# The last image's tail of a selective-scan block, run alone at the end: six pieces at a time, rows kept on chip

## The chip, the cores and the metric

The kernel runs on one core of a Trainium2 chip. The metric is the device time of one execution in microseconds (us), the median of several runs. A profile of one execution shows five engines: PE (matrix products; PEld is its weight load), DVE (vector), ACT (scalar functions), POOL (GpSimd) and SP, which here issues every DMA.

## The reference, cut to what matters

Eight images of 64 x 64 positions and 96 channels go through two layers. Layer 0 is a two-dimensional selective scan: normalise, project to 192 channels, convolve, scan along diagonals and antidiagonals in both directions (16 states for each channel), add the directions, normalise, gate, project back to 96 and add the input. Layer 1 is linear attention over the 4096 positions of an image, then a quantised feed-forward. What the change touches is what comes after the scans:

```python
y01 = ys[:, 0:2] + ys[:, 2:4][..., ::-1]
y = y01[:, 0][..., inv_d] + y01[:, 1][..., inv_a]       # diagonals + antidiagonals
yn = (y - mu) * rsqrt(var + 1e-05) * ln_w + ln_b
x = x + (yn * silu(z)) @ out_proj_w.T                   # layer 0 and its residual
t = x.reshape(8, 4096, 96)
t = t + attention(_ln_t(t))                             # no softmax: q (k^T v), 6 heads
t = t + ffn(_ln_t(t))                                   # 96 -> 384 -> 96, 8-bit floats
```

Since the attention has no softmax, all of it is one 97 x 96 matrix per image, made from the sum over all positions of the outer products of the normalised rows (the gram matrix, with a column of ones). No row can go on before every row of its image has been added to it.

## The kernel before, in words

The scans of the eight images run one after another in a loop over 8 x 16 blocks of 512 positions and 16 states, and use DVE, PE, ACT and POOL at once. Under the scans of image b, generators do the front of image b + 1 (`front`: normalise, convolve, lay out) and the tail of image b - 1 (`tail`). The last image's tail has no scan to lie under: it is put out after the loop, alone.

The order of instructions on each engine is written by a small planner, the class `Work`. A job is a generator; each `yield` names the engine of the next step (A for ACT, V for DVE, G for POOL, P for PE), with its cost and whether it needs a PSUM bank. `next` begins a round and starts the jobs that fit into a phase's width; `at` lets every job whose next step is on this engine put out that step, job after job. In the mode `alone`, which `finish` sets, a round goes through A, V, P and G once, with no regard to costs or due times: the jobs of a phase advance in lockstep, one stage a round, as far as banks go. Engines execute in the order written, so a stage of a later round stands behind the same engine's stages of all jobs of the earlier round.

`tail` has three phases over pieces of 512 positions (`NCH` = 8 pieces an image):

- `join` (L571): loads the two directions' sums y0 and y1 of a piece from the DRAM tensors `wide` (L582), the input rows t (L584) and the gate (L589). PE adds y0 and y1 by products with the identity into PSUM (L597), ACT copies the sum (L604), DVE takes statistics from PSUM (L607, L608). `rsqrt` (L353 to L362) makes scale and shift on ACT and POOL, ACT normalises (L613), PE turns the rows (L619), DVE multiplies by the gate (L621), PE makes the output product with the residual (L625, L633, L636). ACT copies it to t (L640), which is written to the DRAM tensor `mid` (L641). Statistics (L644), root, normalisation by POOL (L652), the gram product (L658) and its sum (L661, L663) follow; the turned rows (L669, L672) go to the DRAM tensor `turned` (L674), whose source lies in y1's buffer. Width 3, and piece c waits until piece c - 2 is through (`joined`). y0 and y1 have three buffers each.
- `attention` (L681): makes the 97 x 96 matrix (L685 to L703).
- `layers` (L710): loads the turned rows (L717) and t (L719) back, adds attention (L722, L727), copies (L731), takes statistics (L735, L736), root, normalises (L742), turns (L747), quantises (L750), makes the hidden layer (L756, ACT L758 and L759), quantises (L762), the second product (L767), copies (L772), and POOL adds (L775, L776). Width 3.

The banks that a tail may use at the end are `banks` (2) and `feed` (3); the three banks of the scans' sum y are not among them. The scans' memory is the pool `scan`, open to the end of the program. The loop ends with `place`, which writes the last block to `wide` (L1036).

The end of `run` before:

```python
work.free += [(f, -9) for f in feed]
work.stream(end(NB - 1))
work.finish(all_done)
```

Of the kernel before, what the change touches and what calls it, by code (L numbers as in the profile page):

```python
# [9 lines left out]
F32 = mybir.dt.float32  # L10
# [3 lines left out]
ALU = mybir.AluOpType  # L14
# [36 lines left out]
@with_exitstack  # L51
def hybrid_block(ctx, tc, x, out, w):


    nc = tc.nc
    NB = x.shape[0]
    const = ctx.enter_context(tc.tile_pool(name="const", bufs=1))
    dram = ctx.enter_context(tc.tile_pool(name="dram", bufs=4, space=DRAM))
    k = weights(tc, const, w)
    pool = ctx.enter_context(tc.tile_pool(name="scan", bufs=1))  # L60
    psum = ctx.enter_context(tc.tile_pool(name="psum", bufs=1, space=PSUM))
    with tc.manual_schedule():

        k.tables = lambda: nc.scalar.preload_act_table_set("natural_log_exp_and_others")
        run(tc, pool, psum, dram, x, out, k, NB)


def weights(tc, const, w):
# [487 lines left out]
        yield [walk(c) for c in range(NST)], 3  # L556


def tail(tc, work, x, out, k, at, b):

    nc = tc.nc
    area = dict(reuse_waits="tile")
    with tc.tile_pool(name=f"t1_{b}", bufs=1, **area) as p1:
        gram = p1.tile([DM + 1, DM + 1], F32, tag="gram", name="gram")
        grams = [0]

        with tc.tile_pool(name=f"t2_{b}", bufs=2, **area) as p2:

            joined = set()

            def join(c):  # L571
                s = slice(4 * c, 4 * c + 4)

                def tile(name, shape, bufs=2):
                    return p2.tile(shape, F32, tag=name, name=name, bufs=bufs)

                ys = [tile(f"y{d}", [P, 4, DI], 3) for d in range(2)]
                for y, src in zip(ys, at.wide):
                    rows = src[0 : HH * WIDE].rearrange("(n y x) -> y n x", y=2, x=WIDE)
                    for v in range(2):  # L580
                        rv = rows[v, s, WW * DI : 2 * WW * DI].rearrange("n (x c) -> x n c", c=DI)
                        nc.sync.dma_start(out=y[v * WW : (v + 1) * WW], in_=rv)  # L582
                t = tile("t", [P, 4, DM], 3)
                nc.sync.dma_start(out=t, in_=x[b].rearrange("(t p) c -> p t c", p=P)[:, s, :])  # L584
                yield "P", 0.0, 4, False
                while c >= 2 and c - 2 not in joined:
                    yield SPIN
                gate = tile("gate", [HC, 2, CH])
                nc.sync.dma_start(out=gate, in_=at.gate[:, :, c * CH : (c + 1) * CH])  # L589
                st, mv = tile("st", [P, 4, 6]), tile("mv", [P, 4, 2])  # L590
                yn = ys[0]
                for j in range(2):
                    ps = yield bank(0.65)
                    v = view(ps, P, 2, DI)
                    for i in range(2):
                        for d in range(2):
                            nc.tensor.matmul(  # L597
                                v[:, i, :], k.ident, ys[d][:, 2 * j + i, :],
                                start=(d == 0), stop=(d == 1), skip_group_check=True,
                            )  # L600
                        if i == 0:
                            yield pe(0.65)
                    yield act(0.5)
                    nc.scalar.copy(yn[:, 2 * j : 2 * j + 2, :], v)  # L604
                    yield dve(1.0, 0)
                    for i in range(2):
                        nc.vector.bn_stats(st[:, 2 * j + i, :], v[:, i, :])  # L607
                        nc.vector.bn_aggr(mv[:, 2 * j + i, :], st[:, 2 * j + i, :])  # L608
                    work.release(ps)
                r, m = yield from rsqrt(nc, p2, k, mv, P, 4, "n")  # L610
                yield act(1.4)
                for i in range(4):
                    nc.scalar.activation(yn[:, i, :], yn[:, i, :], AF.Identity, scale=r[:, i : i + 1], bias=m[:, i : i + 1])  # L613
                yg = tile("yg", [HC, 2, CH])
                for a in range(2):
                    ps = yield bank(0.45)
                    v = view(ps, HC, CH)
                    for i in range(4):
                        nc.tensor.transpose(v[:, i * P : (i + 1) * P], yn[:, i, a * HC : (a + 1) * HC], k.ident)  # L619
                    yield dve(0.7)  # L620
                    nc.vector.tensor_tensor(yg[:, a, :], v, gate[:, a, :], ALU.mult)  # L621
                    work.release(ps)
                ps = yield bank(0.65)
                po = view(ps, P, 4, DM)
                nc.tensor.matmul(  # L625
                    view(ps, P, 4 * DM), k.ident, t.rearrange("p a c -> p (a c)"), start=True, stop=False, skip_group_check=True
                )
                for i in range(4):
                    if i % 2 == 0:
                        yield pe(1.2)  # L630
                    tok = slice(i * P, (i + 1) * P)
                    for a in range(2):
                        nc.tensor.matmul(  # L633
                            po[:, i, :], yg[:, a, tok], k.w_ln[:, a, :], start=False, stop=False, skip_group_check=True
                        )
                        nc.tensor.matmul(  # L636
                            po[:, i, :], gate[:, a, tok], k.b_ln[:, a, :], start=False, stop=(a == 1), skip_group_check=True
                        )
                yield act(0.5)
                nc.scalar.copy(t, po)  # L640
                nc.sync.dma_start(out=at.mid[:, s, :], in_=t)  # L641
                yield dve(1.7, 0)
                for i in range(4):
                    nc.vector.bn_stats(st[:, i, :], po[:, i, :])  # L644
                    nc.vector.bn_aggr(mv[:, i, :], st[:, i, :])
                work.release(ps)
                r, m = yield from rsqrt(nc, p2, k, mv, P, 4, "a")
                xa = ys[0].rearrange("p a c -> p (a c)")[:, 0 : 4 * (DM + 1)].rearrange("p (a c) -> p a c", a=4)
                yield gp(1.6)
                nc.gpsimd.memset(xa[:, :, DM : DM + 1], 1.0)  # L650
                for i in range(4):
                    nc.gpsimd.tensor_scalar(xa[:, i, 0:DM], t[:, i, :], r[:, i : i + 1], m[:, i : i + 1], ALU.mult, ALU.add)  # L652


                ps = yield bank(0.65)
                v = view(ps, DM + 1, DM + 1)
                for i in range(4):
                    nc.tensor.matmul(v, xa[:, i, :], xa[:, i, :], start=(i == 0), stop=(i == 3))  # L658
                yield dve(0.3)
                if grams[0] == 0:  # L660
                    nc.vector.tensor_copy(gram, v)  # L661
                else:
                    nc.vector.tensor_tensor(gram, gram, v, ALU.add)  # L663
                grams[0] += 1
                work.release(ps)
                ps = yield bank(0.45)
                v = view(ps, DM + 1, CH)
                for i in range(4):
                    nc.tensor.transpose(v[:, i * P : (i + 1) * P], xa[:, i, :], k.ident)  # L669
                xaT = ys[1].rearrange("p a c -> p (a c)")[0 : DM + 1, 0:CH]  # L670
                yield act(0.6)
                nc.scalar.copy(xaT, v)  # L672
                work.release(ps)
                nc.sync.dma_start(out=at.turned[:, c * CH : (c + 1) * CH], in_=xaT)  # L674
                joined.add(c)

            yield [join(c) for c in range(NCH)], 3

        att = SimpleNamespace()

# [24 lines left out]

        yield [attention()], 1

        with tc.tile_pool(name=f"t3_{b}", bufs=3, **area) as p2:

            def layers(c):  # L710
                s = slice(4 * c, 4 * c + 4)

                def tile(name, shape, dtype=F32):
                    return p2.tile(shape, dtype, tag=name, name=name)

                xaT = tile("xaT", [DM + 1, CH])
                nc.sync.dma_start(out=xaT, in_=at.turned[:, c * CH : (c + 1) * CH])  # L717
                t = tile("t", [P, 4, DM])
                nc.sync.dma_start(out=t, in_=at.mid[:, s, :])  # L719
                ps = yield bank(0.65, 4)  # L720
                po = view(ps, P, 4, DM)
                nc.tensor.matmul(  # L722
# [53 lines left out]
                nc.gpsimd.tensor_tensor(t, t, y16, ALU.add)  # L776
                nc.sync.dma_start(out=out[b].rearrange("(t p) c -> p t c", p=P)[:, s, :], in_=t)

            yield [layers(c) for c in range(NCH)], 3


def run(tc, pool, psum, dram, x, out, w, NB):

# [4 lines left out]


    nc = tc.nc
    steps = [
        (b, q, c) for b in range(NB) for q in range(2) for c in (range(NST) if q == 0 else range(NST - 1, -1, -1))
    ]
# [291 lines left out]
    for i in range(total + LAG + 1):  # L1087
# [34 lines left out]
        if i + 4 < total:  # L1122
            fetch(i + 4)
        feeds.pop(i, None)
    work.free += [(f, -9) for f in feed]
    work.stream(end(NB - 1))
    work.finish(all_done)


# [75 lines left out]
```

## Time and profile before

| | us |
|---|---|
| median of 3 runs | 12146.02 |
| lowest, highest | 12140.42, 12148.66 |
| the profiled execution | 12157.04 |
| its span, first to last instruction | 12155.1 |

| engine | busy us | share of the span |
|---|---|---|
| PE | 9958.7 | 82% |
| PEld | 8012.1 | 66% |
| DVE | 9683.1 | 80% |
| ACT | 9501.2 | 78% |
| POOL | 9737.6 | 80% |

How to read the lines below. The slices cut the span in 40 equal parts; a digit is the busy share in tenths, PEclk the TensorE clock that was granted, in tenths of full speed. A line of the timeline has the start in us, the time, the engine, the line of the code, the operation, out<-in, shapes and count. A line of the chain of waits has the start, the time and what the chain was in. A line of the stage windows has a stretch, its length, busy us (and instructions) of PE, PEld, DVE, ACT and POOL, then the granted clock (1.00 is full), the DMA engines' busy share and GB/s.

### The profile page before, as it was taken

To read this page: it belongs to the slowest core of one execution; us is meant where nothing else is said; L and a number is where in the kernel's file an instruction comes from. 1 tells how busy PE (TensorE), PEld (TensorE's weight loads), DVE (VectorE), ACT (ScalarE), POOL (GpSimd) and SP (SyncE) were. 2 spreads that over 40 slices of the span, in tenths; PEclk is the share of its full clock that TensorE was granted. 3 is DMA by queue.
4 is the path that set the end of the run, shared out by engine and by line. 5 is a ranking of instruction groups with operands and counts; after the bars stand their busy time and mean duration, and the time that the engine had idled before them with its cause. 6 is when DMAs were issued, how large, how long until landed. Compare 5 with 4: busy or idle time off the path is not lost.

```text
span 12155.1 us, 187007 instructions
## 1 busy us (share of the span) xinstructions
PE 9958.7 (82%) x62804; PEld 8012.1 (66%) x62804; DVE 9683.1 (80%) x11092; ACT 9501.2 (78%) x19842; POOL 9737.6 (80%) x6927
## 2 busy tenths in 40 slices
PE   4698889888898888988888888988889888888874
PEld 3476667666676666766677666766667666666653
DVE  1488998878888888888888888888888878888971
ACT  1588888877888788877888878887788878878862
POOL 0588998878988788888888889888898888889972
PEclk9799999998998989989899999999989899988985
DMA  2334333533335433353333433344333443322331
GB/s 53 91 92 124 100 93 94 136 104 96 94 88 134 112 94 93 90 141 101 95 90 106 127 102 95 90 127 117 92 92 93 132 108 93 100 87 84 100 93 42
DMA packets 1138471, 1213.47 MB, mean 100 GB/s; under 512 B 464998, under 2 KB 744167, under 8 KB 1137511
## 3 DMA queue, kind: packets, MB, share of 16 engines
q1 hardware_dynamic: 1137510, 1201.51, 36.0%
q8 instruction: 499, 8.18, 0.3%
q14 instruction: 462, 3.78, 0.1%
HBM read 877.94 MB, written 323.09 MB: 99 GB/s over the span
## 4 chain that ended last, share of the span: by engine, by line
PE 29%; ACT 22%; DVE 20%; POOL 11%; issue 9%; SPq 4%; DMA 4%; DVEq 0%; POOLq 0%; ACTq 0%
DVE h L958 13%; ACT feedT L937 8%; PE y L993 7%; PE feed L945 7%; ACT decay L923 6%; POOL h L979 6%; DVE feed L962 4%; PE bank L493 3%; DMA cc<-crow 2%; PE bank L835 2%; SPq L538 2%; PE bank L877 1%; POOL delta L874 1%; PE feed L947 1%; PE bank L858 1%
## 5 line engine op out<-in xcount | busy, mean ns | idle before, releaser
L979 POOL TENSOR_TENSOR h<-h,cc 128x1536 f32<-128x1536 f32 x2048 | 7073.1, 3454 | 401.7 <-DMA cc<-crow 205.0
L958 DVE TENSOR_TENSOR_SCAN h<-decay,carry,feed 128x512 f32<-128x512 f32 x5376 | 6500.6, 1261 | 623.0 <-PE feed L945 510.4
L923 ACT ACTIVATE decay<-delta,a_neg 128x512 f32<-128x512 f32 x6144 | 3976.8, 713 | 1303.6 <-DVE h L958 1298.1
L945 PE MATMUL feed<-ident,feedT 128*128 128x128 f32 x15360 | 2738.5, 303 | 1508.3 <-DVE h L958 1237.9
L993 PE MATMUL y<-ident,h 128*128 128x128 f32 x24576 | 3804.4, 289 | 68.6 <-ACT ys L1021 37.3
L937 ACT ACTIVATE feedT<-duT,rows 128x192 f32<-128x192 f32 x10240 | 3670.8, 443 | 1.6 <-PE feed L945 1.1
L993 PEld LDWEIGHTS y<-ident,h 128*128 128x128 f32 x24576 | 3154.2, 151 | 527.5 <-issue 483.4
L945 PEld LDWEIGHTS feed<-ident,feedT 128*128 128x128 f32 x15360 | 1970.4, 155 | 2118.5 <-DVE h L958 667.9
L962 DVE TENSOR_TENSOR feed<-feed,du 128x512 f32<-128x512 f32 x2304 | 1442.5, 687 | 210.7 <-PE feed L947 205.8
L974 POOL COPY carry<-h 128x3 f32<-128x3 f32 x2048 | 395.4, 193 | 1065.4 <-DVE h L958 985.8
L958 DVE TENSOR_TENSOR_SCAN h<-decay,feed 128x512 f32<-128x512 f32 x768 | 883.9, 1202 | 102.5 <-PE feed L945 83.2
L493 PE MATMUL bank<-wf,xp 97*128 97x192 f32 x4320 | 873.6, 334 | 1.7 <-ACT xp L458 1.7
L947 PE MATMUL feed<-x,pick 77*128 77x512 f32 x1536 | 846.4, 633 | 0.7
L493 PEld LDWEIGHTS bank<-wf,xp 97*128 97x128 f32 x4320 | 704.8, 195 | 28.8 <-issue 15.9
L879 DVE SCALAR_TENSOR_TENSOR delta<-bank,delta 128x512 f32<-128x512 f32 x381 | 258.5, 678 | 287.0 <-POOL delta L874 159.6
L886 POOL TENSOR_TENSOR du<-delta,u 128x1536 f32<-128x1536 f32 x128 | 449.4, 3511 | 10.6 <-DVE delta L879 10.6
L877 PE MATMUL bank<-x,ws 13*128 13x512 f32 x762 | 439.4, 657 | 20.8 <-DVE delta L879 20.8
L872 POOL TENSOR_TENSOR e<-e,duT 128x1536 f32<-128x1536 f32 x128 | 441.9, 3452 | 16.7 <-ACT delta L865 16.6
L858 PE MATMUL bank<-x,ws 13*128 13x512 f32 x766 | 436.6, 650 | 17.3 <-ACT x L848 17.3
L874 POOL TENSOR_TENSOR delta<-delta,e 128x1536 f32<-128x1536 f32 x128 | 441.0, 3446 | 0.1
L947 PEld LDWEIGHTS feed<-x,pick 77*128 77x128 f32 x1536 | 261.0, 201 | 152.7 <-issue 96.2
L835 PE MATMUL bank<-wx,u 128*128 128x77 f32 x3048 | 356.5, 273 | 0.0
(260 smaller groups left out, 8885.1 us busy)
## 6 DMA issues: line engine op xcount, KB each, us to landing
cc<-crow SPq DMA_DIRECT2D x4096, 128.0 KB
u<-seq SPq DMA_DIRECT2D x256, 384.0 KB
wide<-ys SPq DMA_DIRECT2D x512, 192.0 KB
ut<-image SPq DMA_DIRECT2D x768, 64.0 KB
seq<-us SPq DMA_DIRECT2D x128, 384.0 KB
part<-ys SPq DMA_DIRECT2D x64, 768.0 KB
y<-part SPq DMA_DIRECT2D x64, 768.0 KB
y<-wide SPq DMA_DIRECT2D x256, 192.0 KB
```

The lines of the kernel that those rows point to most:

```text
L493: nc.tensor.matmul(v[:, j, :], flat[:, o : o + P], k.wf[:, i, :], start=(i == 0), stop=(i == 8), skip_group_check=True)
L835: nc.tensor.matmul(v[:, j, :], u[:, g, j * P : (j + 1) * P], w.wx[:, q, g, :], start=(g == 0), stop=(g == G - 1))
L874: nc.gpsimd.tensor_tensor(delta, delta, e, ALU.add)
L877: nc.tensor.matmul(ps, w.ws[:, q, g, :], x[0 : 2 * NR + 1, :], start=True, stop=True)
L923: nc.scalar.activation(decays[i][:, g, :], made[m].delta[:, g, :], AF.Exp, scale=w.a_neg[:, q, g, n : n + 1])
L937: nc.scalar.activation(f[part], o.duT[part], AF.Copy, scale=scale)
L945: nc.tensor.transpose(feed[g][:, j * P : (j + 1) * P], feeds[i][:, j * G + g, :], w.ident)
L947: nc.tensor.matmul(feed[0], w.pick[:, FEED[:n].count("D"), :], made[m].x, start=True, stop=True)
L958: nc.vector.tensor_tensor_scan(h[:, g, back], a[:, g, back], feed[g][:, back], init, ALU.mult, ALU.add)
L962: nc.vector.tensor_tensor(feed[g], feed[0], made[m].du[:, g, :], ALU.mult)
L979: nc.gpsimd.tensor_tensor(hs[i], hs[i], c.unsqueeze(1).to_broadcast([P, G, T]), ALU.mult)
L993: nc.tensor.matmul(y[:, j, :], hs[i][:, g, r * P : (r + 1) * P], w.ident, is_transpose=True, start=(n == 0 and j % 4 == 0), stop=(n == NS ...
```

## The change

The last image's tail is called with `last=True`, after the scans' pool is closed, and differs in this:

- `join` and `layers` run at width 6 with six buffers, without the wait for piece c - 2; `join` starts at DVE's step at once, and a piece loads y0, y1, t and its gate in this order.
- The directions are added by DVE from memory, in place in y0, and the statistics are taken there; L597 and L604 are not put out.
- t and the turned rows of all eight pieces stay on chip (`kept`); `mid` and `turned` are neither written nor read.
- The scans' sum y gives three more banks: eight in all.

The tails of the other images are as before.

```diff
-    pool = ctx.enter_context(tc.tile_pool(name="scan", bufs=1))
...
-def tail(tc, work, x, out, k, at, b):
+def tail(tc, work, x, out, k, at, b, last=False):
...
+        kept = {}
-        with tc.tile_pool(name=f"t2_{b}", bufs=2, **area) as p2:
+        with tc.tile_pool(name=f"t2_{b}", bufs=6 if last else 2, **area) as p2:
...
-                t = tile("t", [P, 4, DM], 3)
+                t = p1.tile([P, 4, DM], F32, tag=f"t{c}", name="t") if last else tile("t", [P, 4, DM], 3)
...
-                yield "P", 0.0, 4, False
-                while c >= 2 and c - 2 not in joined:
+                if not last:
+                    yield "P", 0.0, 4, False
+                while not last and c >= 2 and c - 2 not in joined:
                     yield SPIN
...
-                for j in range(2):
+                if last:
+                    yield dve(2.5)
+                    nc.vector.tensor_tensor(yn, ys[0], ys[1], ALU.add)
+                    for i in range(4):
+                        nc.vector.bn_stats(st[:, i, :], yn[:, i, :])
+                        nc.vector.bn_aggr(mv[:, i, :], st[:, i, :])
+                for j in range(0 if last else 2):
...
-                nc.sync.dma_start(out=at.mid[:, s, :], in_=t)
+                if not last:
+                    nc.sync.dma_start(out=at.mid[:, s, :], in_=t)
...
-                xaT = ys[1].rearrange("p a c -> p (a c)")[0 : DM + 1, 0:CH]
+                if last:
+                    xaT = p1.tile([DM + 1, CH], F32, tag=f"xaT{c}", name="xaT")
+                else:
+                    xaT = ys[1].rearrange("p a c -> p (a c)")[0 : DM + 1, 0:CH]
...
+                if last:
+                    kept[c] = t, xaT
+                else:
+                    nc.sync.dma_start(out=at.turned[:, c * CH : (c + 1) * CH], in_=xaT)
...
-            yield [join(c) for c in range(NCH)], 3
+            yield [join(c) for c in range(NCH)], 6 if last else 3
...
-        with tc.tile_pool(name=f"t3_{b}", bufs=3, **area) as p2:
+        with tc.tile_pool(name=f"t3_{b}", bufs=6 if last else 3, **area) as p2:
...
+                if last:
+                    t, xaT = kept[c]
+                else:
...
-            yield [layers(c) for c in range(NCH)], 3
+            yield [layers(c) for c in range(NCH)], 6 if last else 3
...
+    scans = ExitStack()
+    pool = scans.enter_context(tc.tile_pool(name="scan", bufs=1))
...
-    work.free += [(f, -9) for f in feed]
-    work.stream(end(NB - 1))
+    work.finish(all_done)
+    scans.close()
+    y = psum.tile([P, TB * G, P], F32, tag="y", name="y_end").rearrange("p (b k) c -> p b (k c)", b=G)
+    work.free += [(f, -9) for f in feed] + [(y[:, g, :], -9) for g in range(G)]
+    work.stream(tail(tc, work, x, out, w, image(NB - 1), NB - 1, True))
     work.finish(all_done)
```

More of the change, by code (lines that the diff above doesn't have):

```diff
@@ L64, in hybrid_block @@
         k.tables = lambda: nc.scalar.preload_act_table_set("natural_log_exp_and_others")
-        run(tc, pool, psum, dram, x, out, k, NB)
+        run(tc, psum, dram, x, out, k, NB)
 def weights(tc, const, w):
@@ L574, in tile @@
                 def tile(name, shape, bufs=2):
-                    return p2.tile(shape, F32, tag=name, name=name, bufs=bufs)
+                    return p2.tile(shape, F32, tag=name, name=name, bufs=6 if last else bufs)
                 ys = [tile(f"y{d}", [P, 4, DI], 3) for d in range(2)]
@@ L590, in join @@
                 st, mv = tile("st", [P, 4, 6]), tile("mv", [P, 4, 2])
+                yg = tile("yg", [HC, 2, CH]) if last else None
                 yn = ys[0]
-                for j in range(2):
+                if last:
[5 more added lines that the diff above has]
+                for j in range(0 if last else 2):
                     ps = yield bank(0.65)
@@ L613, in join @@
                     nc.scalar.activation(yn[:, i, :], yn[:, i, :], AF.Identity, scale=r[:, i : i + 1], bias=m[:, i : i + 1])
-                yg = tile("yg", [HC, 2, CH])
+                yg = yg or tile("yg", [HC, 2, CH])
                 for a in range(2):
@@ L673, in join @@
                 work.release(ps)
-                nc.sync.dma_start(out=at.turned[:, c * CH : (c + 1) * CH], in_=xaT)
+                if last:
+                    kept[c] = t, xaT
+                else:
+                    nc.sync.dma_start(out=at.turned[:, c * CH : (c + 1) * CH], in_=xaT)
                 joined.add(c)
-            yield [join(c) for c in range(NCH)], 3
+            yield [join(c) for c in range(NCH)], 6 if last else 3
         att = SimpleNamespace()
@@ L714, in tile @@
                     return p2.tile(shape, dtype, tag=name, name=name)
[L716 to L719, printed above, removed]
+                if last:
+                    t, xaT = kept[c]
+                else:
+                    xaT = tile("xaT", [DM + 1, CH])
+                    nc.sync.dma_start(out=xaT, in_=at.turned[:, c * CH : (c + 1) * CH])
+                    t = tile("t", [P, 4, DM])
+                    nc.sync.dma_start(out=t, in_=at.mid[:, s, :])
                 ps = yield bank(0.65, 4)
@@ L777, in layers, with run @@
                 nc.sync.dma_start(out=out[b].rearrange("(t p) c -> p t c", p=P)[:, s, :], in_=t)
-            yield [layers(c) for c in range(NCH)], 3
-def run(tc, pool, psum, dram, x, out, w, NB):
+            yield [layers(c) for c in range(NCH)], 6 if last else 3
+def run(tc, psum, dram, x, out, w, NB):
     nc = tc.nc
+    scans = ExitStack()
+    pool = scans.enter_context(tc.tile_pool(name="scan", bufs=1))
     steps = [
```

## The prediction

> **What bounds the kernel now.** The page's forty slices come first; one slice is 12155.1 / 40 = 304 us.
>
> ```profile
> PE   4698889888898888988888888988889888888874
> DVE  1488998878888888888888888888888878888971
> PEclk9799999998998989989899999999989899988985
> ```
>
> From the second slice to the third last, scans keep DVE, PE, ACT and POOL 70 to 90% busy. In the last slice DVE is busy a tenth and the TensorE clock is at half: the last image's tail runs there alone, and there no engine is the limit. The timeline of SP's queue and of POOL dates it.
>
> ```profile
> 11779.32 6.39 SPq L1036 DMA_DIRECT2D wide<-ys  x8
> 11785.88 3.76 SPq L582 DMA_DIRECT2D y<-wide  x4
> ...
> 11823.37 1.64 POOL L652 TENSOR_SCALAR y<-t,ar,am 128x96 f32<-128x96 f32 x4
> ...
> 11827.09 1.64 POOL L652 TENSOR_SCALAR y<-t,ar,am 128x96 f32<-128x96 f32 x4
> ...
> 11977.88 0.24 ACT L703 COPY w_att<-feed 97x96 f32<-97x96 f32 x1 [1.29 <-PE feed L700]
> ```
>
> The scans' last result leaves at 11779, the tail's first load is issued at 11785.9, the attention matrix is ready at 11978.1, the span ends at 12155.1. So `join` with the attention takes 192 us and `layers` 177: 369 us, 3% of the span, and the change touches nothing else. POOL takes 3.72 us a piece for the second normalisation (11823.37 to 11827.09). Next, the chain inside this stretch:
>
> ```profile
> 11881.37 10.16 DMA turned<-y
> 11891.55 0.57 SPq L582
> ...
> 11925.42 10.18 DMA turned<-y
> 11935.62 0.57 SPq L582
> ...
> 11995.13 16.64 DMA t<-mid
> ...
> 12056.10 17.32 DMA t<-mid
> ...
> 12110.27 16.47 DMA t<-mid
> ```
>
> Two of `join`'s four pairs wait 10 us for the write of `turned` before their own y loads may start (y1 holds the turned rows). Each of the three groups of `layers` first waits for `mid` and `turned` to come back. Why so long? The stage windows (us; PE, PEld, DVE, ACT, POOL busy; clock, DMA share, GB/s):
>
> ```profile
> 11794.00:11796.00 2.00, 1.91 (x6) 1.43 (x6) 0.00 (x0) 0.45 (x1) 0.00 (x0) 0.50 1.14 230
> ...
> 11830.00:11832.00 2.00, 2.00 (x10) 2.00 (x9) 0.00 (x0) 1.17 (x2) 0.00 (x0) 0.50 0.01 3
> 11832.00:11834.00 2.00, 2.00 (x12) 2.00 (x11) 0.20 (x1) 0.48 (x1) 0.00 (x0) 0.84 0.07 13
> ...
> 11836.00:11838.00 2.00, 0.00 (x0) 0.00 (x0) 0.14 (x1) 0.00 (x0) 0.19 (x1) 1.00 0.07 26
> ...
> 11868.00:11870.00 2.00, 2.00 (x11) 2.00 (x11) 0.00 (x0) 0.00 (x0) 0.00 (x0) 0.50 0.00 0
> ...
> 11872.00:11874.00 2.00, 2.00 (x9) 1.49 (x8) 1.32 (x8) 0.44 (x1) 0.00 (x0) 0.60 0.27 98
> ```
>
> While `turned` (97 rows, 194 KB) moves, the DMA share is 0.07, about one engine of 16, at 26 GB/s; y loads reach 230. So the waits that the chain puts down to `mid` are largely the 97-row transfers ahead of it in SP's queue. The clock column matters too: at 11868 PE shows busy throughout, at half clock.
>
> **The change, part by part.** From the first scan to the last `place` nothing changes: the second `finish` finds nothing left (image 6's tail has no instruction after 11300), so I cost it at nothing. Closing the scans' memory adds waits at tiles that overlap it; their last readers are done by 11779 but for `ys`, whose write the y load follows anyway. If that cover is gone, the first load is some 3 us later.
>
> Removed: 8 writes and 8 loads each of `mid` and `turned`, with their issues in SP's queue. No queued transfer is moved past another except the first loads, now in order y, t, gate per piece. Removed per piece too: 16 PE records of L597 (0.25 to 0.43 us each) and two ACT copies (0.48). Added per piece: one DVE add 128x768 from memory. No such row exists; the nearest is L621, 96x512 at 0.69, or 0.95 by length. Floor is 0.69, ceiling 1.4, I take 0.95; statistics add four times 0.47. Together 2.9 us, the loads' rate covering the first five.
>
> In lockstep every stage is issued for all six pieces before the next, so an engine's stage k+1 waits for its piece 5 in stage k. I walk this through (pieces 0 to 7, times from the span's start).
>
> `join`, six pieces. A piece loads 768 + 192 + 384 KB = 1.376 MB; at the 238 GB/s of 11790 to 11804 that is 5.8 us. Piece 0's y were complete at 11793.2, so piece 5's are at 11822. DVE 2.9 and waits: 11825. Ln and Exp 0.6, then ACT's six normalisations at 1.95 (L613: 1.86 and a gap): 11837.5, PE's first transposes beside them. Second transposes, six times 4: 5 us, 11843. Output products (L625, L633, L636), six: each 4.05 us at full clock, 8.1 at half.
>
> [...] The row: in 11862 to 11872 these products ran at clock 0.50 for 10 us of busy PE and did not raise it; only the next transposes did. [...] The change idles PE from 11778 until about 11826. [...] by the row it can stay cold: 48.6. But 24 dense transposes now come first, and the like (gram, transposes, sums from 11828) raised the clock to 0.84 at 11832. I take a warm entry, 24.3, and keep 48.6 for the range: 11867.5.
>
> Copy, Ln and Exp 1.1, then POOL 6 x 3.72 = 22.3: 11891. Statistics lie beside PE and POOL.
>
> Pieces 6 and 7. Their y0 buffers come free at the third transposes, about 11892.3; a load took 4.9 us (11891.5 to 11896.4), the second 3.8 more: 11901. DVE 2.9, ACT 0.6 and 3.9, transposes 2.5: 11911. Products 6 + 4 (half warm): 11921. Copy and root 1.1, POOL 7.4: 11929.5. Gram and attention 6.2, as before (POOL's end 11971.9 to 11978.1): 11935.7. `join` gains 42 us.
>
> `layers`, six pieces, no load. First products (L722, L727) take 3.4 us a piece cold and about half of it warm; dense now, so 5 us cold and the rest warm, 14 (ceiling 20.5): 11949.7. Copy and root 1.1, POOL 22.3: 11973.1. A gap of 1.0, then ACT's copy and relu, 18 x 1.24 (nine took 11.15) = 22.3: 11996.4. A copy 0.5, POOL's sums 6 x 1.86: 12008. PE does pieces 6 and 7's first products meanwhile. POOL 7.2 for their normalisation: 12015.3. From there to the end of span 16.8, as in the last group before (12138.3 to 12155.1): 12032. `layers` and the rest take 96 us instead of 177.
>
> Sum: 12155.1 - 12032 = 123 us. The profiled execution took 12157.04 us, 11 above the median of the runs (12146.02); the saving is a difference inside one stretch, so I take it from the median: 12023 us.
>
> **The rivals.** (1) PE stays cold. For: the clock is 0.50 through all of `layers`. Against: bursts get six pieces long. Products 24.3 more, the second pair's 6, transposes 1.4, first products 6.5: saving 85, 12061 us.
>
> (2) The gain is only that of the removed round trips, since six-deep barriers give back what depth wins in `join`. The three waits in `layers` are 34 us (11978 to 12011.8), 28 (12045.5 to 12073.5) and 19.5 (12107.3 to 12126.9), which is all that the walk gains there; two of 10 us in `join`, less some 15 for a first load of six instead of three pieces, make 86 in all: 12060. For: POOL and ACT stages grow in proportion to the pieces. Against: in `join` the old pairs left every engine idle a third of the time or more.
>
> (3) Slower: the load convoy. All 8.26 MB of six pieces are issued at once and the whole first group waits for piece 5. At 238 GB/s this is 35 us; it eats the whole 123 at 8.26 MB / 158 us = 52 GB/s and makes the kernel slower below that, 12155 at 49. For: 24 GB/s are seen in `layers`. Against: those are the 97-row transfers; y, t and gate loads ran at 230 and more side by side.
>
> (4) The program does not get the overlap: shared buffers force the pieces apart (banks, y buffers). With six buffers, eight banks and one bank a piece per stage I see no such wait; 12146 if so.
>
> **How the numbers follow.** The walk as laid out 0.66 (12005 to 12045); rival 1 0.15; rival 2 0.13; rival 3 0.03; rival 4 0.03. A measurement of this kernel tells about 0.2%, 24 us, from no change. The first three are beyond that: faster 0.94, same 0.03, slower 0.03. The range goes from 12003 (warm from the first product on in `layers`, a quicker add, loads at 250 GB/s and shorter gaps: 20 more) to 12063, which takes in rivals 1 and 2.
>
> **What would show it.** Right: attention's copy near 11936 and the end near 12032; no DMA `mid` or `turned` for the last image; DVE add at about 0.95 us; POOL's L652 groups six in a row at 3.72; ACT's relu 18 in a row; clock 1.00 during the first six products. Wrong: those at 0.42 us a pair (clock 0.50), piece 5's y after 11830, or the first load later than 11789.

## The result, and the profile after

The changed kernel took 12034.65 us (median of 4 runs, 12030.84 to 12038.08), the kernel before 12143.22 us beside it (4 runs, 12137.3 to 12148.66): ratio 0.9911, 95% interval 0.9893 to 0.9928. That is 109 us less by the medians, and 87 to 130 us by the interval. The forecast was 12023, within 12003 to 12063. By the two profiled spans the saving is 12155.1 - 12030.3 = 124.8 us.

The slices of the page after show the same loop of scans and another last slice: DVE has 3 where it had 1, and the clock is 0.6 instead of 0.5.

```profile
DVE  1488998888888888888888888888888878878893
PEclk9799999999999989989899998999999999988996
```

The timeline after (start, time, engine, line, operation) dates the tail. The span ends at 12030.3.

```profile
11782.20 3.80 SPq L584 DMA_DIRECT2D y<-wide  x4
...
11866.44 1.64 POOL L663 TENSOR_SCALAR y<-t,ar,am 128x96 f32<-128x96 f32 x4
11870.15 1.64 POOL L663 TENSOR_SCALAR y<-t,ar,am 128x96 f32<-128x96 f32 x4
...
11935.57 0.24 ACT L720 COPY w_att<-feed 97x96 f32<-97x96 f32 x1 [1.29 <-PE feed L717]
```

"Tail" below is the time from the issue of the last image's first y load to the end of the span; `join` with attention ends at the copy of `w_att`, and `layers` is the rest. Before: 192.2 + 177.0 = 369.2 us. After: 153.6 + 94.5 = 248.1 us. Those 121.1 us are the change; the other 3.7 of the spans' difference lie ahead of the first load (11785.9 and 11782.2), in code that the change leaves alone.

The chain of waits after (start, time, what) has no `turned` and no `mid`. What it waits for now are loads of y and "issue", time in which an engine waited for nothing that the chain can name:

```profile
11789.34 5.53 DMA y<-wide
...
11894.35 5.97 DMA y<-wide
...
11969.89 24.00 issue
...
12012.95 10.46 issue
```

What these are is seen in the stage windows, cut where one engine hands over to the next (stretch, length, busy us and instructions of PE, PEld, DVE, ACT, POOL; clock, DMA share, GB/s):

```profile
11782.20:11822.20 40.00, 0.00 (x0) 0.00 (x0) 16.67 (x54) 2.91 (x12) 7.08 (x36) 0.50 1.02 217
11822.20:11838.10 15.90, 14.52 (x47) 7.52 (x48) 6.14 (x10) 10.62 (x25) 1.18 (x6) 0.53 0.00 1
11838.10:11864.20 26.10, 25.61 (x207) 23.86 (x205) 8.50 (x43) 2.65 (x7) 0.19 (x1) 1.00 0.01 1
11864.20:11887.40 23.20, 11.20 (x50) 9.47 (x51) 2.22 (x12) 2.39 (x13) 18.17 (x71) 0.58 0.00 0
...
11947.00:11969.90 22.90, 9.50 (x23) 3.59 (x23) 7.02 (x34) 3.19 (x13) 17.95 (x65) 0.56 0.00 0
11969.90:11993.50 23.60, 13.25 (x71) 6.55 (x71) 6.68 (x8) 21.72 (x37) 0.00 (x0) 0.50 0.00 1
11993.50:12005.60 12.10, 4.69 (x44) 3.84 (x42) 3.79 (x17) 4.31 (x12) 11.12 (x12) 0.78 0.30 81
```

In each stretch shown one resource is busy for most of the time and most of the rest stand about: the DMA engines for 40 us (share 1.02), then PE (25.61 of 26.10), POOL (18.17 of 23.20), and in `layers` POOL, ACT (21.72 of 23.60) and POOL again. The 24 us of "issue" in the chain are ACT's hidden layer of six pieces, for which POOL waits. The tail is still a sequence of stages, now each for six pieces.

### The profile page after: what moved, and what is told of

Its sections match the earlier page's. It is cut to its first block, busy times and chain, and to the rows that moved or that the text cites. A ratio compares the mean times of both kernels' runs of the same rounds, so it can differ in the third digit from the quotient of the medians.

```text
span 12030.3 us, 186634 instructions
## 1 busy us (share of the span) xinstructions
PE 9894.5 (82%) x62676; PEld 7964.4 (66%) x62676; DVE 9687.6 (81%) x11100; ACT 9491.9 (79%) x19826; POOL 9736.6 (81%) x6927
## 4 chain that ended last, share of the span: by engine, by line
PE 31%; DVE 21%; ACT 21%; POOL 11%; issue 9%; SPq 4%; DMA 3%; DVEq 0%; POOLq 0%; ACTq 0%
DVE h L980 13%; ACT feedT L959 8%; PE y L1015 7%; PE feed L967 7%; POOL h L1001 6%; ACT decay L945 6%; DVE feed L984 4%; PE bank L492 4%; DMA cc<-crow 2%; PE bank L857 2%; SPq L537 2%; PE bank L899 2%; POOL delta L896 1%; PE feed L969 1%; POOL e L894 1%
```

## The experiments

The theory after the result: nearly all of the gain is the removed round trips of `mid` and `turned`, and what makes those dear is that a transfer of 97 rows keeps about one DMA engine of 16 busy (share 0.07). The rival: the gain is depth, six pieces with their buffers and eight banks. Two questions came later: what the order of the pieces costs, and what the banks do. The letters in the expectations belong to each run alone.

Tails are from one profile each. The same kernel profiled twice gave tails 4.0 us (experiment 5) and 0.3 us apart (8), and the same tail code in two kernels gave tails 9.8 us apart (6 and 7), so a difference of less than some 10 us between two tails decides nothing. A time without an interval is a single run; the kernel before took 12141.9 us beside the first four (one run), 12157.28 (median of 7 runs) beside those of experiments 6 and 7 and the first of 5, 12153.3 (one run) beside the first of 8, and 12153.91 (median of 7 runs) beside the repeats in 5 and 8.

### 1. Only the rows kept on chip (kernel before)

```diff
+    scans.close()
+    work.stream(tail(tc, work, x, out, w, image(NB - 1), NB - 1, True))
...
+                t = p1.tile([P, 4, DM], F32, tag=f"t{c}", name="t") if last else tile("t", [P, 4, DM], 3)
...
+                if last:
+                    kept[c] = t, xaT
+                else:
+                    nc.sync.dma_start(out=at.turned[:, c * CH : (c + 1) * CH], in_=xaT)
```

Width 3, five banks, the sums by PE and the waits of the pairs stay as before.

> The kernel before with one part of the change: the last image's residual and turned rows stay on chip (the scans' pool is closed ahead of the tail for the room); width 3, five banks and PE's sums of the directions as before. The tail, from its first y load's issue to the end of span, took 369 us before and 248 after. Theory A (the gain is the removed round trips of mid and turned): layers falls by 81 of its 177 us (three load waits of 34, 28 and 19.5), join by 20 to 30 (10 us at a pair's border), the tail is 255 to 268. Rival B (depth and banks carry it): half of the gain or less, the tail is 305 or more.

Measured: 12034.3 us, as much as the whole change took; tail 164.4 + 92.9 = 257.3 us. Of the tail's 121 us this part alone brings 112. In its chain of waits only the y loads of the later pairs are left, at 4 us, without the 10 us for `turned` ahead of them:

```profile
11822.81 4.10 DMA y<-wide
...
11860.72 3.52 DMA y<-wide
```

So the removed round trips are nearly all of the gain. `layers` takes 92.9 us here (width 3, five banks) and 94.5 us in the changed kernel (width 6, eight banks): with nothing to load, depth and banks together bring nothing there.

### 2. Only the size of the transfer (kernel before)

```diff
-                nc.sync.dma_start(out=at.turned[:, c * CH : (c + 1) * CH], in_=xaT)
+                wide = ys[1].rearrange("p a c -> p (a c)")[0:112, 0:CH]
+                nc.sync.dma_start(out=at.turned[:, c * CH : (c + 1) * CH], in_=wide)
...
-                xaT = tile("xaT", [DM + 1, CH])
+                xaT = tile("xaT", [112, CH])
...
+                xaT = xaT[0 : DM + 1]
...
-                turned=dram.tile([DM + 1, L], F32, tag="turned", name=f"turned_{b}"),
+                turned=dram.tile([112, L], F32, tag="turned", name=f"turned_{b}"),
```

`turned` gets 112 rows, of which 15 are never used, and is written with 112 too, in all eight images. Every round trip stays.

> The kernel before with one size changed: turned and its chip rows have 112 rows instead of 97 (15 more rows of no meaning travel along); all transfers stay. Theory A1 (the 97-row transfers run on one DMA engine of 16, DMA share 0.07, and that is what the waits are made of): a transfer takes 1 to 3 us instead of 9 or 10, each wait in layers shrinks to 4 to 8 us, the two waits of 10 us in join to 3, the tail is 275 to 295. Rival A2 (it is the round trip through DRAM itself, whatever the shape): the tail stays within 360 to 375.

Measured: 12046.7 us; tail 166.6 + 117.6 = 284.2 us. More bytes, and a tail 85 us shorter. The chain's three waits in `layers` (16.64, 17.32 and 16.47 us in the kernel before) are now:

```profile
11924.01 4.10 DMA t<-mid
...
11967.67 3.25 DMA t<-mid
...
12009.67 3.73 DMA t<-mid
```

The prediction's window has a share of 0.07 and 26 GB/s while the 97 rows of `turned` moved. This window of the run, in which a `turned` of 112 rows is written, has 0.67 and 201 GB/s:

```profile
11918.50:11919.50 1.00, 0.00 (x0) 0.00 (x0) 0.00 (x0) 0.00 (x0) 0.77 (x5) 0.50 0.67 201
```

That is nearly ten times the share and nearly eight times the rate, and 0.67 of 16 engines is about 11, far beyond one. Why 112 rows keep so many more engines busy than 97 is not shown; only these two sizes of `turned` were run. With `mid` untouched its waits fell to a quarter or less, so what the profile had put down to `mid` was mostly the 97-row transfers in front of it.

### 3. The sums by PE again (kernel after)

```diff
-                if last:
-                    yield dve(2.5)
-                    nc.vector.tensor_tensor(yn, ys[0], ys[1], ALU.add)
...
-                for j in range(0 if last else 2):
+                for j in range(2):
```

> The changed kernel with one part undone: the directions are again added by PE into PSUM (16 products and two ACT copies a piece, statistics from PSUM). Tail 248 us with DVE's add. Theory A (DVE's add lies under the loads, PE's sums cost two more lockstep stages behind piece 5's load): six pieces' second sums 12 to 20 us behind the load, 4 to 8 in the second group: tail 262 to 278. Rival C (the add is no gain, since PE enters warm from its own sums): 243 to 252.

Measured: 12050.6 us; tail 174.6 + 95.7 = 270.3 us, 22 us longer than after, all but one of it in `join`. In lockstep PE's sums and ACT's copies of six pieces are another stage in the row, while DVE's add of 0.96 us runs beside the loads: the six normalisations begin 55.8 us after the first load here (11834.23), and 40.0 us after it in the changed kernel.

### 4. Width 3 with the rest of the change (kernel after)

```diff
-            yield [join(c) for c in range(NCH)], 6 if last else 3
+            yield [join(c) for c in range(NCH)], 3
...
-            yield [layers(c) for c in range(NCH)], 6 if last else 3
+            yield [layers(c) for c in range(NCH)], 3
```

> The changed kernel with width 3 in both phases, six buffers, eight banks and all else kept. Theory A (depth six itself gives nothing, since each stage's sum over the pieces is the same and the first group waits for its last piece's load): join 140 to 150 instead of 153.6 (next group's loads come early), layers 92 to 97 instead of 94.5: tail 232 to 247. Rival B (depth carries it): tail 265 or more.

Measured: 12012.6 us; tail 140.5 + 101.2 = 241.7 us, 6.4 less than at width 6: 13.1 gained in `join`, 6.7 lost in `layers`. (`layers` came out longer than theory A had it, 92 to 97.) By the expectation the rival needed 265 us or more, so the depth of six is not what the change gains by. Whether it costs anything is not shown: 6.4 us is within what one profile can differ from another.

### 5. Five banks instead of eight (kernel after), twice

```diff
-    y = psum.tile([P, TB * G, P], F32, tag="y", name="y_end").rearrange("p (b k) c -> p b (k c)", b=G)
-    work.free += [(f, -9) for f in feed] + [(y[:, g, :], -9) for g in range(G)]
+    work.free += [(f, -9) for f in feed]
```

> The changed kernel with one part undone: the tail has the five banks of before, not eight. Tail 248 us with eight. Theory A (in lockstep of six every piece wants a bank in the same stage; the sixth gets none for some rounds and its chain trails): 256 to 275. Rival D (banks are never short, the engines' sums set the pace): 246 to 252.

Measured: 12007.4 us; tail 143.5 + 83.3 = 226.8 us, 21 less than after, against both expectations. The same kernel again, timed:

> The changed kernel with five banks, timed in several runs (its single time was 12007 us, the changed kernel's four runs 12031 to 12038). If the five banks' gain is real, the ratio to the kernel before is 0.988 to 0.990 and the profile's tail 220 to 235; if that single look was luck, for instance of the clock, 0.991 and 245 to 250.

Measured: 12011.26 us (4 runs, 12006.02 to 12015.14), ratio to the kernel before 0.9882 (0.9867 to 0.9897); tail 142.1 + 88.7 = 230.8 us. So it repeats in the tail, and the times agree, though the two intervals of the ratios still touch. ACT's timeline of the first of these runs (in brackets, how long ACT sat idle and for what) has the normalisation of the first group and two copies of the output product, of the group's fifth and sixth piece:

```profile
11819.94 10.60 ACT L623 ACTIVATE y<-y,nm,nr 128x192 f32<-128x192 f32 x24
...
11854.81 0.48 ACT L650 COPY t<-feed 128x384 f32<-128x384 f32 x1 [3.74 <-PE feed L646]
...
11882.83 0.48 ACT L650 COPY t<-feed 128x384 f32<-128x384 f32 x1 [3.61 <-PE feed L646]
```

All six pieces are normalised together (24 operations in one row). The fifth piece's output product is copied at 11854.81, the sixth's only 28.0 us later: it gets no bank, drops out of the lockstep, and goes on with pieces 6 and 7. The other five need not wait for it: the last of their turned rows is copied at 11879.2, 100.3 us after the first load. In the kernel after, the last of six is copied at 11892.8, 110.6 us after it, and then every engine starts on pieces 6 and 7 together. The granted clock is not the difference in `join`: it is 0.64 there in both (0.66 in the repeat). So the trace suggests that fewer banks acted as a change of order; where `layers` got its other 6 to 11 us was not traced. The next runs test the order itself.

### 6. Eight pieces, in lockstep and staggered (kernel after)

First width 8 with eight buffers, still in lockstep:

```diff
-            yield [join(c) for c in range(NCH)], 6 if last else 3
+            yield [join(c) for c in range(NCH)], 8 if last else 3
...
```

> The changed kernel with width 8 and eight buffers instead of six: all pieces in one lockstep group. Theory A (stages of a lockstep group are barriers, so the sum of the stages stays and only the second group's own latency goes; the first stage now waits for piece 7's load, 12 us later): join 145 to 152, layers 92 to 97: tail 238 to 250. Rival B (depth carries it): 225 or less.

Measured: 12022.0 us; tail 149.7 + 97.1 = 246.8 us, as after within 1.3 us. Then the same with piece c put c rounds of the planner later, in `join` and in `layers`:

```diff
+                    for _ in range(c):
+                        yield SPIN
                     yield dve(2.5)
...
                     t, xaT = kept[c]
+                    for _ in range(c):
+                        yield SPIN
```

> The changed kernel with width 8, eight buffers, and piece c starting c rounds late in both phases (the stages of different pieces then alternate in each engine's order). Theory A (lockstep barriers and the wait for the last load are what is left): join falls to the load of 46 us plus a piece's latency and PE's sums, 95 to 125; layers to 65 to 80; tail 160 to 205, time 0.6% below the changed kernel. Rival E (the rounds' own latency, with every engine waiting in turn, costs as much as the barriers): tail 235 to 260.

Measured: 11958.72 us (4 runs, 11957.66 to 11962.9), the kernel before 12157.28 beside it, ratio 0.984 (0.9824 to 0.9857); tail 102.2 + 67.1 = 169.2 us. Nothing computed, loaded or allotted differs between these two kernels: the order in which the engines get the instructions is worth 78 us of the tail, the clock that goes with it included. (The times differ by 63 us, since the first load came 14.7 us later in the staggered profile.) The windows of the two halves of the tail, first width 8 in lockstep, then staggered (columns as above):

```profile
11773.40:11923.10 149.70, 75.89 (x443) 62.09 (x444) 45.64 (x160) 30.36 (x84) 36.01 (x153) 0.65 0.37 77
11923.10:12020.20 97.10, 49.02 (x232) 28.03 (x230) 23.70 (x80) 38.92 (x81) 38.97 (x104) 0.59 0.06 17
```

```profile
11788.00:11890.00 102.00, 70.22 (x443) 62.13 (x443) 44.37 (x160) 29.93 (x83) 39.73 (x153) 0.72 0.54 113
11890.00:11957.40 67.40, 39.83 (x233) 27.20 (x232) 25.67 (x80) 39.75 (x81) 42.99 (x104) 0.65 0.09 24
```

The instruction counts are equal within two. PE is busy 51% of `join` in lockstep (75.89 of 149.70) and 69% staggered (70.22 of 102.00); POOL in `layers` goes from 40% to 64%. DVE's and ACT's busy times hardly move. PE's fall by 6 and 9 us, with the higher clock beside them, which is far less than 78: most of the gain is overlap.

### 7. Staggered, with 112 rows for the other seven images

The kernel of 6 with the sizes of 2, which act here only in images 0 to 6, under the scans.

> The staggered kernel, and for the other seven images turned has 112 rows instead of 97. Theory A (those tails lie under scans, whose loads share SP's queue with the one-engine transfers): the first y load of the last tail comes 10 to 25 us earlier than with 97 rows (it came at 11760 with 112 rows and 11769 to 11786 without), the total falls by the same. Rival F (that spread is the runs' own, the transfers are hidden): total within 10 us of the staggered kernel's.

Measured: 11936.74 us (4 runs, 11933.86 to 11941.92), ratio 0.9822 (0.9807 to 0.9836): 22.0 us less than in 6. So the slow transfers cost something under the scans too; by which wait was not traced. The first load of the last tail is issued at 11754.5 instead of 11788.2, 33.7 us earlier and more than the 10 to 25 expected, but that is one profile each: the kernels with 97 rows have it anywhere from 11769 to 11788, those with 112 rows from 11754 to 11775. The tail itself was 9.8 us longer (179.0), in code that is the same. Windows of 10 us, of the kernel of 6 from 80 to 90 us after its first load, then of this one from 80 to 100:

```profile
11868.20:11878.20 10.00, 7.62 (x70) 7.10 (x68) 3.18 (x15) 2.49 (x6) 4.07 (x15) 1.00 0.00 0
```

```profile
11834.50:11844.50 10.00, 8.03 (x46) 7.20 (x45) 2.64 (x12) 1.31 (x4) 3.56 (x14) 0.60 0.01 2
11844.50:11854.50 10.00, 10.00 (x54) 9.78 (x53) 1.66 (x10) 1.75 (x6) 3.08 (x12) 0.54 0.00 0
```

With the clock at 1.00 PE put through 70 products in 7.62 us; at 0.60 it took 8.03 us for 46, and at 0.54 it was busy all the time for 54 (the stretches need not hold the same products). Over the tail PE's busy time is 119.21 us against 110.05, for the same instructions. The lower clock goes with the 10 us; what moves the clock was not isolated.

### 8. Staggered, 112 rows and five banks, twice

> The staggered kernel with 112 rows, and five banks instead of eight in the last tail. Theory A2 (five banks helped the changed kernel only by putting its sixth piece out of step; once the pieces are out of step there is nothing to gain, and at most five of eight pieces want a bank in one round anyway): tail within 165 to 190, as the 169 and 179 of the two staggered kernels. Rival D2 (fewer banks are quicker by themselves, for instance by the order in which they come free): 150 or less. Rival D3 (banks bind once the pieces overlap): 195 or more.

Measured: 11918.1 us; tail 92.7 + 64.1 = 156.8 us. Again, timed:

> The staggered kernel with 112 rows and five banks, timed (single look 11918 us, tail 157; with eight banks 11934 to 11942 in four runs, tail 179). If five banks are quicker out of step too, ratio 0.980 to 0.981 and tail 150 to 162 again; if the difference was the clock's luck, the runs spread over 11915 to 11945 and the tail lies nearer 165 to 180.

Measured: 11929.53 us (4 runs, 11922.88 to 11941.15), ratio 0.9816 (0.9799 to 0.9832); tail 92.8 + 64.3 = 157.1 us. The tail is 22 us shorter than in 7, twice, and repeats to 0.3 us; in total the kernel is not told apart from 7, since the intervals of the ratios overlap and the first load came later than in 7 (at 11759.5 and 11774.6). The windows of `join`, of 7, then of the two runs of 8:

```profile
11754.50:11864.70 110.20, 77.94 (x443) 69.25 (x444) 44.49 (x160) 30.20 (x84) 39.86 (x153) 0.67 0.51 104
```

```profile
11759.50:11852.20 92.70, 67.55 (x443) 60.74 (x444) 44.26 (x160) 30.24 (x84) 39.45 (x153) 0.76 0.59 124
```

```profile
11774.60:11867.40 92.80, 67.85 (x443) 60.91 (x444) 44.33 (x160) 30.23 (x84) 39.68 (x153) 0.76 0.60 124
```

The same instructions take PE 10 us less at a clock of 0.76 instead of 0.67, and `join` is 17.5 us shorter. Banks and clock go together here, so which of the two does it stays open; the first tail lies between two of the expectations (165 to 190 us, and 150 at most), the second within its own (150 to 162). By the medians the kernels of 7 and 8 are 0.8 to 0.9% faster than the changed one, and the fastest of all.

## Why the prediction held, and where its reasons did not

**The time.** By its walk the saving was 123 us; the spans differ by 124.8, the medians by 109. The walk was a difference of profiles. The profiled execution before lay 11 us above its median, which the prediction took to fall out of the difference; it did not fall out wholly. The part ahead of the tail differs from profile to profile (with the 97 rows, the first load lay anywhere from 11769 to 11788), by more than the 16 us between the two savings. The range, 12003 to 12063, took in rivals 1 and 2 as well, so the time alone could not tell the walk from them.

**The steps of `join`,** each from its first load. Piece 5's add starts 36.6 us after it (36.1 by the walk). It and the six normalisations together in the timeline after:

```profile
11818.79 0.96 DVE L598 TENSOR_TENSOR y<-y,y 128x768 f32<-128x768 f32 x1 [2.92 <-DMA y<-wide]
11822.22 10.60 ACT L623 ACTIVATE y<-y,nm,nr 128x192 f32<-128x192 f32 x24
```

The add takes 0.96 us, as the estimate by length from L621's 0.69 us had it (0.95). ACT takes 10.60 us for six pieces, 1.77 each instead of 1.95. PE entered the products warm: the window from 11838.10 has clock 1.00, and six pieces took 25.6 us (24.3 in the walk), so rival 1 fell. Ahead of that PE was busy 14.52 of 15.90 us at a mean clock of 0.53. These were the transposes that were to bring the clock up: from their start at 11822.8 to 11837.0 it stood at 0.50, over 13.4 us of busy PE, more than the 10 us of the prediction's row, and from 11837.5 on at 1.00. The warm entry came, but how soon it would come was the author's estimate. POOL's spacing is 3.71 us, as before. Pieces 6 and 7 were a little dearer: the second's y came 6 us behind the first's, not 3.8. `w_att` is ready after 153.6 us; the walk had 149.8.

**The steps of `layers`.** First products 11.5 us (14 in the walk; the mean clock was 0.83), POOL 22.3, ACT 22.5, POOL's sums 11.6, the end 248.1 us after the first load; the walk had 246.1. Every stage is within 4 us of its term.

**The reason that failed.** The prediction gave rival 2, "the gain is only that of the removed round trips, since six-deep barriers give back what depth wins in `join`", 0.13 and 86 us. As to the cause this rival was nearly right, and its size was off: the kept rows bring 112 us of the tail by themselves (experiment 1), 84 in `layers` and 28 in `join`. For `layers` the walk agrees, since it says itself that the three load waits are all that it gains there. What it had wrong is `join`: of its 42 us only 20, two waits of 10, were put down to the round trips. There was a third wait, at the first border between pairs. SP stood 8.18 us at the issue of one gate load, ahead of the next y loads, while the DMA share was 0.07:

```profile
11832.23 8.18 SPq L589 DMA_DIRECT2D gate<-gate  x1
```

With the rows kept, none of the eight gate loads takes more than 0.58 us to issue (0.57 each in the changed kernel). Rival 2 also charged 15 us for a first load of six pieces, which a kernel at width 3 does not have.

The walk arrived at the right time because it followed each stage of the six-deep order, which was right; what depth and the rest bring in `join` is 11 us (164.4 to 153.6), not 22. Against the kept rows alone, the rest of the change nets 9 us of the tail, no more than two profiles of the same tail code differed by, and nothing in the time (12034.3 and 12034.65). Its pieces, each by its own run: the add by DVE gains 22 us, eight banks lose 17 to 21, width 6 loses 6 at most. They are taken out of the full change one at a time and need not add up.

**What it missed.** It took eight banks for free of any cost (rival 4: "I see no such wait") and never asked whether the order itself was the limit. Lockstep was: 78 of the remaining 248 us. Rival 3, the convoy of slow loads, did not come about: the first 40 us ran at 217 GB/s. Rival 4 did not either. And the prediction noticed the share of 0.07 for the 97 rows without asking what 112 rows would do, which turned out to be 85 of the 121 us for a change of a size.

## What to carry to other kernels

When a wait for a small transfer is long, look at the DMA share beside it before removing the transfer: 0.07 is about one engine of 16, and here a padded row count (112 for 97) brought 85 of the 121 us. Giving every piece the same stage at the same time made this tail a sum of stages (PE 25.61 of 26.10 us, then POOL 18.17 of 23.20). Eight buffers instead of six did not shorten that sum (1.3 us) and eight banks instead of five lengthened it, while offsetting the pieces by a round each took 78 us off. A forecast whose total is right has not shown its reason: take the change apart and time the parts.

## What the runs showed of the hardware that was not expected

- Adding 15 rows of no use to a 97-row transfer shortened a tail by 85 us, and the same edit to transfers that run beside the scans shortened the kernel by 22 us by the medians (4 runs each).
- The same tail code, with another history ahead of it, ran at a clock of 1.00 in one kernel and 0.54 to 0.60 in another, with PE busy up to all of the stretch, and took 10 us longer.
- With three banks fewer the lockstep tail was 17 to 21 us shorter, and the staggered one 22 us shorter, there with a clock of 0.76 instead of 0.67 in `join`.
